# A graph layer and a mixture of experts on one core: row loads three blocks ahead, a bias add on VectorE, later router steps

## The chip, the cores and the metric

The kernel runs on one core of one Trainium2 chip. The metric is device time in microseconds (us) for one execution of the whole program; lower is better. Short names of engines, as the profile has them: PE is TensorE's matmul, PEld its weight load, DVE is VectorE, ACT is ScalarE, POOL is GpSimd, SP is SyncE (here it only issues DMAs and loads registers). L764 is line 764 of the kernel before.

## The reference

All data are float32. `x` has 6250 nodes of 256 features; 100000 edges with 96 features each are sorted by target node `dst`.

```python
# message passing and MLP, on h0 = layernorm(x)
out1 = segment_sum(edge_attr, dst, n)
out2 = where(cnt > 0, segment_max(edge_attr, dst, n), 0)
out3 = out1 / maximum(cnt, 1)
h = concatenate([h0, out1, out2, out3, u[0] for each node], axis=1)
h = relu(h @ W1 + b1) @ W2 + b2          # hidden size 1024, out 256
x = x + (h + h0)
# mixture of experts, on g = layernorm(x)
topk_vals, topk_idx = top_k(g @ gate_w + gate_b, 2)          # 16 experts
w = softmax(topk_vals)
moe = sum over the two chosen e of w_e * (relu(g @ w1[e] + eb1[e]) @ w2[e] + eb2[e])   # inner size 512
y = g + moe
x = x + layernorm(y) * gamma + beta
```

## The kernel before

**Groups and slots.** Nodes lie in 50 tiles of 125; four tiles make a group, 13 groups in all (group 0 has two tiles). A group is worked on in 12 slots. The order of all instructions is written by a planner: `at_slot(T, fn, ..., cost)` puts a step into slot T, the steps are then emitted in the order of their slots, and each engine works through its own queue in that order. In a slot PE has eight first-layer matmul parts (`hidden`, L764) or a second-layer output (`output`, L792). A slot of 4.6 us of VectorE time is filled up with pieces of the edge stream; the `cost` of a step is taken from what the stream may use. In the terms of the code, a step at `B + k` of group g lies in slot 12 g + k.

**Edge stream.** Chunks of edge columns are loaded by SP (`raw`, L176), VectorE runs a segmented sum and maximum over them (L316, L317, L319, L320, one 125x768 instruction each for a column), and SP stores the result (`rows_d`, L329). When a region of edges is done, `chain_runs` carries runs across rows and partitions: VectorE (L385 to L396), PE transposes (L404, L406), VectorE scans (L415 to L421), PE transposes (L430), VectorE (L436, L438), and a store of `carry_d` on GpSimd's queue (L440). A group's slot needs its region's edges first (`edges_until`).

**A group's way.** `take_x` loads its nodes, `stats_x`, `root_x`, `scale_x`, `norm_x` make the layer norm; `keep_x` scales `xt` on ScalarE (L714) and adds the second bias `b2b` on GpSimd (L716); `take_edges` and `take_carry` gather segment results with indirect DMAs of GpSimd (L722, L729); VectorE joins them (L735, L737), ScalarE masks them (L742); `turn` transposes on PE (L755). Then `hidden`, `output`, and `residual` on VectorE (L797). The router: `turn_b` (PE, L822), `logits` (PE, L830), `choose` (VectorE, L837 on), `rank` (VectorE, L851 to L858), `rank_2` (PE, L865 and L866), `place` (VectorE, L874 to L887) and `send`, eight indirect stores of GpSimd a group, which put each node's row into `xg_d` once for each of its two experts (L891). The PSUM pool `pG` that `logits`, `rank_2` and `bounds` use has one buffer.

**Bounds.** `bounds(b)` finds where each node's edges end: two VectorE instructions on sums that ScalarE made (L502), then two PE matmuls (L516, L517). It is called for parts of the nodes, before they are needed.

**Expert blocks.** 57 blocks of 256 rows are run one after the other; the first 14 belong to the most chosen expert and share one set of weights, the others have weights of their own (1026 KB each). `load_block(b)` has SP load two registers, the rows `xb` (L1028), and for most blocks the expert's second bias `eb` (L1033) and weights `wt` (L1035); buffers: seven for `xb`, three for weights. `run_block(b)` emits: `weigh` of block b-1 (VectorE L1077, ScalarE L1079, store of `y_d` on SP, L1081), `load_block(b+2)`, `finish` of an older block, four first-layer steps on PE (L1152) with relu on ScalarE (L1158), between them `turn_block(b+1)` (PE L1048), partners' rows gathered from `y_d` by GpSimd (L1090), statistics on VectorE, `norm_y`, and `norm_block(b+2)` on ScalarE, which is the first to read `xb` (L1041); last the second layer on PE (L1176). The last group's sends are emitted between the first blocks: two tiles' before block 5, two tiles' before block 6.

Of the kernel before, what the change touches and what calls it, by code (L numbers as in the profile page):

```python
# [14 lines left out]
OP = mybir.AluOpType  # L15
# [4 lines left out]
P = 125  # L20
PA = 80
RR = 8
GW = 2
# [14 lines left out]
SLOTS = 12  # L38
# [7 lines left out]
def kernel(  # L46
# [460 lines left out]
    def bounds(b):  # L507

        a, z = node_cols(b)
        n = z - a  # L510
        cols = slice(a, z)
        nc.vector.tensor_scalar(rp[:, cols], acc2[:, cols], float(KB), 0.5, op0=OP.add, op1=OP.mult)
        nc.vector.scalar_tensor_tensor(rp[:, cols], blk_f[:, cols], float(KB), rp[:, cols], op0=OP.mult, op1=OP.add)

        ends[b] = ps_e = pGp.tile([P, GS * NE], F32, name="pg")
        nc.tensor.matmul(ps_e[:, :n], sh, rp[:, cols], start=True, stop=False)  # L516
        nc.tensor.matmul(ps_e[:, :n], wrap, rp[:, a + 1:z + 1], start=False, stop=True)  # L517
# [191 lines left out]
    def keep_x(g):  # L709

        n = GRP[g][1] - GRP[g][0]
        xt = G[g]["xt"]
        for i in range(n):
            nc.scalar.activation(xt[:, i, 0:D], xt[:, i, 0:D], AF.Identity, scale=G[g]["rs1"][:, i:i + 1],  # L714
                                 bias=G[g]["nb"][:, i:i + 1])
        nc.gpsimd.tensor_tensor(xt[:, :n, 0:D], xt[:, :n, 0:D], b2b[:, None, :].to_broadcast([P, n, D]), op=OP.add)  # L716

# [202 lines left out]
    def open_experts():  # L920
# [3 lines left out]
        MB["pools"] = pools = ExitStack()  # L924
        for nm, bufs in (("tb", 1), ("wp", 3), ("xg", 7), ("bk", 3), ("yb", 4)):
            MB[nm] = pools.enter_context(tc.tile_pool(name=nm, bufs=bufs, side="right"))
# [91 lines left out]

    def load_block(b):
        if b < NA:  # L1020
            r = nc.sync.value_load(MB["tab_a"][0:1, b:b + 1], min_val=0, max_val=(NA - 1) * SB)
            e = nc.sync.value_load(star_i[0:1, 0:1], min_val=0, max_val=NE - 1) if b == 0 else None
        else:
            e = nc.sync.value_load(MB["tab"][0:1, 0, b - NA:b - NA + 1], min_val=0, max_val=NE - 1)
            r = nc.sync.value_load(MB["tab"][0:1, 1, b - NA:b - NA + 1], min_val=0, max_val=NE * N - SB)
        BL[b]["r"] = r
        BL[b]["xb"] = xb = MB["xg"].tile([128, 2, DR], F32, name="xb")
        nc.sync.dma_start(xb, xg_d[ds(r, SB), :].rearrange("(p h) d -> p h d", h=2))  # L1028
        if 0 < b < NA:
            BL[b]["wt"], BL[b]["eb"] = BL[0]["wt"], BL[0]["eb"]  # L1030
            return
        BL[b]["eb"] = eb = MB["wp"].tile([128, D], F32, name="eb")
        nc.sync.dma_start(eb, eb2[ds(e, 1), :].to_broadcast([128, D]))  # L1033
        BL[b]["wt"] = wt = MB["wp"].tile([128, WROW], F32, name="wt")
        nc.sync.dma_start(wt, wpack[ds(e * 128, 128), :])  # L1035
# [96 lines left out]
    def run_due(kind, fn, keep):  # L1132
        while len(due[kind]) > keep:
            fn(due[kind].pop(0))

    def run_block(b, end):
        xT, wt = BL[b]["xT"], BL[b]["wt"]
        run_due("weigh", weigh, 0)
        if b + 2 < end and "wt" not in BL[b + 2]:
            load_block(b + 2)  # L1140
        run_due("finish", finish, 0)
# [80 lines left out]
    for g, (a, z) in enumerate(GRP):  # L1222
        B, n = SLOTS * g, z - a
        if g:
# [9 lines left out]
            for i in range(n):  # L1234
# [4 lines left out]
                else:  # L1239
# [6 lines left out]
                    at_slot(min(2 * i + 5, SLOTS - 2), mean_window, g, i)  # L1246
            at_slot(B - (4 if g == GW else 7), keep_x, g)
            for k in range(DC):
                at_slot(B - (4 if g == GW else 6) + k, turn, g, k)
# [8 lines left out]
        at_slot(B + SLOTS + 1 - early, root_b, g)  # L1258
        at_slot(B + SLOTS + 2 - early, scale_b, g, cost=0.3)
        for k in range(DC):  # L1260
            at_slot(B + SLOTS + 1 + k, turn_b, g, k)
        at_slot(B + SLOTS + 3, logits, g)
        at_slot(B + SLOTS + 4, choose, g, cost=2.4)
        at_slot(B + SLOTS + 5, rank, g, cost=1.3)
        at_slot(B + SLOTS + 6, rank_2, g)
        at_slot(B + SLOTS + 7, place, g, cost=1.5)
        for i in range(n):
            at_slot(B + SLOTS + 8 + i // 2, send, g, i)
    T = SLOTS * (NG - 3) + 21
# [3 lines left out]
    for b in range(3):  # L1273
        at_slot(T + 4 + b, load_block, b)
    T = SLOTS * (NG - 1) + HC + GRP[-1][1] - GRP[-1][0]
# [11 lines left out]
    for b in range(GW, len(IB)):  # L1287
# [10 lines left out]
        T = max(0, SLOTS * sum(IB[:b]) - (9 if b == GW else 12))  # L1298
        at_slot(T, bounds, b, cost=0.4)
        at_slot(T + 1, index_nodes, b, cost=4.0)  # L1300
# [3 lines left out]
    def fill_rows():  # L1304

        nc.vector.memset(fill[:, D + 1:D + 5], 4.0 * NE * N)
        for h in range(SB // 128):
            nc.gpsimd.dma_start(xg_d.rearrange("(e n) d -> n e d", n=N)[h * 128:(h + 1) * 128],
                                fill[:, None, :].to_broadcast([128, NE, DR]))

    at_slot(4, fill_rows)
    at_slot(6, find_star)
# [107 lines left out]
    with tc.manual_schedule():  # L1420
        global_part()
        stats_x(0, 0)
        for t in reversed(range(a, z)):
            find_edge(t)
        bounds(0)
        index_windows(0)
        for i in range(z - a):
# [6 lines left out]
        norm_x(0)  # L1434
        bounds(1)
        index_windows(1)
        for h in range(2):
# [57 lines left out]
    with tc.If(nc.values_load(MB["more"][0:1, 0:1]) != 0):  # L1495
        with tc.manual_schedule():
            for b in range(NS, min(NB, NS + 3)):
                load_block(b)
            for b in range(NS, min(NB, NS + 2)):
# [44 lines left out]
```

## Time and profile before

| | |
|---|---|
| three runs | 1319.05, 1316.25, 1308.22 us; median 1316.25 |
| profiled execution | 1312.53 us; span 1310.6 us, mean granted PE clock 0.946 |
| busy share of the span | PE 86%, PEld 60%, DVE 74%, ACT 47%, POOL 46% |
| DMA | 261.25 MB, mean 199 GB/s |
| chain that ended last | PE 28%, DVE 25%, DMA 16%, issue 11%, ACT 6%, POOL 6%, SP 4% |
| largest waits | ACT L1041 for `xb`: 105.9 us; POOL L716 for ACT L714: 57.2 us |

A busy share is a mean over stages that have different limits, so the table says little about any one stage. A view by stretches of time tells which engine is full where. A line of groups or of the timeline has: start and length in us (timeline only), engine, source line, operation, tile written and tiles read, shape, count, and in square brackets the idle time of the engine just before, with what ended it. Matmul ends are modelled; starts are recorded.

### The profile page before, as it was taken

To read this page: it belongs to the slowest core of one execution; us is meant where nothing else is said; L and a number is where in the kernel's file an instruction comes from. 1 tells how busy PE (TensorE), PEld (TensorE's weight loads), DVE (VectorE), ACT (ScalarE), POOL (GpSimd) and SP (SyncE) were. 2 spreads that over 40 slices of the span, in tenths; PEclk is the share of its full clock that TensorE was granted. 3 is DMA by queue.
4 is the path that set the end of the run, shared out by engine and by line. 5 is a ranking of instruction groups with operands and counts; after the bars stand their busy time and mean duration, and the time that the engine had idled before them with its cause. 6 is when DMAs were issued, how large, how long until landed. Compare 5 with 4: busy or idle time off the path is not lost.

```text
span 1310.6 us, 16927 instructions
## 1 busy us (share of the span) xinstructions
PE 1125.1 (86%) x4637; PEld 788.1 (60%) x4637; DVE 970.5 (74%) x2741; ACT 617.8 (47%) x1449; POOL 602.0 (46%) x734
## 2 busy tenths in 40 slices
PE   2584696988989888999979999988999899999892
PEld 1353363646556454655636567866888777888771
DVE  4569787989989989999988522534468777888775
ACT  3474342643547442353333422422466666666662
POOL 4131152773578574637444513030045455564654
PEclk9897798998999888999998999998999999999996
DMA  5949775698699988899997221221577788888872
GB/s 162 216 110 229 216 220 156 182 299 230 176 236 274 251 251 217 223 264 236 267 268 195 67 82 33 65 82 49 181 214 227 231 255 257 263 243 259 259 254 73
DMA packets 179475, 261.25 MB, mean 199 GB/s; under 512 B 35915, under 2 KB 145963, under 8 KB 173729
## 3 DMA queue, kind: packets, MB, share of 16 engines
q1 hardware_dynamic: 140241, 202.23, 54.5%
q0 software_dynamic: 39008, 57.35, 15.8%
q8 instruction: 40, 0.66, 0.2%
q14 instruction: 74, 0.61, 0.1%
q10 hardware_dynamic: 112, 0.41, 0.1%
HBM read 146.70 MB, written 122.01 MB: 205 GB/s over the span
## 4 chain that ended last, share of the span: by engine, by line
PE 28%; DVE 25%; DMA 16%; issue 11%; ACT 6%; POOL 6%; SPq 4%; POOLq 0%; DVEq 0%; ACTq 0%
PE acc L1176 9%; PE acc L1152 8%; DMA rows_d<-rw 6%; PE acc L764 5%; DVE rw L317 3%; PE acc L792 3%; DMA xb<-xg_d 3%; DVE rw L320 3%; DMA xt<-in_x_dram 2%; DVE rw L319 2%; DVE rw L316 2%; ACT yb L1079 2%; POOL xg_d L891 2%; DVE yb L1077 2%; SPq L176 2%
## 5 line engine op out<-in xcount | busy, mean ns | idle before, releaser
L764 PE MATMUL acc<-inT,w1x 128*128 128x500 f32 (+1 forms) x832 | 375.2, 602 | 11.8 <-ACT hT L786 10.1
L764 PEld LDWEIGHTS acc<-inT,w1x 128*128 128x128 f32 x832 | 164.2, 205 | 175.2 <-issue 155.0
L1152 PE MATMUL acc<-xT,wt 128*128 128x256 f32 x912 | 224.3, 389 | 26.8 <-ACT hb L1158 22.2
L891 POOL DMA_INDIRECT xg_d<-xt,pos_i x100 | 156.7, 1567 | 160.5 <-DVE xt L887 87.7
L1176 PE MATMUL acc<-wt,hb 128*128 128x256 f32 x912 | 207.8, 381 | 0.0
L1152 PEld LDWEIGHTS acc<-xT,wt 128*128 128x128 f32 x912 | 169.8, 192 | 60.2 <-ACT hb L1158 35.7
L1176 PEld LDWEIGHTS acc<-wt,hb 128*128 128x128 f32 x912 | 174.7, 192 | 24.3
L792 PE MATMUL acc<-w2s,hT 128*125 128x256 f32 x800 | 180.8, 382 | 0.0
L792 PEld LDWEIGHTS acc<-w2s,hT 128*125 128x125 f32 x800 | 148.6, 189 | 23.0 <-issue 1.9
L1090 POOL DMA_INDIRECT g<-y_d,from_i x86 | 89.7, 1043 | 130.1 <-DMA y_d<-yb 94.0
L1123 POOL DMA_INDIRECT out_dram<-g,to_i x86 | 89.6, 1042 | 101.1 <-ACT hb L1158 77.2
L1041 ACT ACTIVATE xnb<-xb 128x256 f32<-128x256 f32 x114 | 62.1, 593 | 108.1 <-DMA xb<-xg_d 105.9
L495 POOL DMA_INDIRECT gb<-in_dst_dram,blk_i x50 | 72.8, 1456 | 85.8 <-DVE blk_i L492 44.4
L1158 ACT ACTIVATE hb<-acc,wt 128x256 f32<-128x256 f32 x200 | 87.8, 465 | 49.5 <-PE acc L1152 34.3
L786 ACT ACTIVATE hT<-acc,c 128x500 f32<-128x500 f32 (+1 forms) x104 | 60.3, 662 | 96.3 <-PE acc L781 96.3
L1077 DVE TENSOR_TENSOR yb<-acc,xe 128x512 f32<-128x512 f32 x57 | 39.4, 691 | 87.0 <-PE acc L1176 57.0
L756 ACT COPY inT<-pT 128x500 f32<-128x500 f32 (+1 forms) x65 | 36.4, 560 | 106.8 <-PE pT L755 91.1
L316 DVE TENSOR_TENSOR rw<-rw,keep 125x768 f32<-125x768 f32 x81 | 76.8, 949 | 12.3 <-DMA rows_d<-rw 9.5
L320 DVE TENSOR_TENSOR rw<-rw,raw 125x768 f32<-125x768 f32 x88 | 85.6, 972 | 0.0
L319 DVE TENSOR_TENSOR rw<-rw,raw 125x768 f32<-125x768 f32 x88 | 83.4, 948 | 0.0
L722 POOL DMA_INDIRECT at<-rows_d,first_i x44 | 60.9, 1385 | 46.8 <-issue 25.5
L317 DVE TENSOR_TENSOR rw<-rw,bar 125x768 f32<-125x768 f32 x81 | 81.3, 1004 | 0.0
(313 smaller groups left out, 1623.6 us busy)
## 6 DMA issues: line engine op xcount, KB each, us to landing
wt<-in_wpack_dram SPq DMA_DIRECT2D x44, 1026.0 KB
rows_d<-rw SPq DMA_DIRECT2D x46, 960.0 KB
rows_d<-rw SPq DMA_DIRECT2D x46, 540.0 KB
raw<-in_edge_dram SPq DMA_DIRECT2D x46, 480.0 KB
xb<-xg_d SPq DMA_DIRECT2D x57, 263.0 KB
y_d<-yb SPq DMA_DIRECT2D x57, 256.0 KB
raw<-in_edge_dram SPq DMA_DIRECT2D x46, 270.0 KB
xt<-in_x_dram SPq DMA_DIRECT2D x12, 500.0 KB
```

The source lines that it names most:

```text
L316: nc.vector.tensor_tensor(su, prev[0], keep[c][:, :, s + j, None].to_broadcast(bcast), op=OP.mult)
L317: nc.vector.tensor_tensor(mx, prev[1], bar[c][:, :, s + j, None].to_broadcast(bcast), op=OP.min)
L319: nc.vector.tensor_tensor(su, su, x_j, op=OP.add)
L320: nc.vector.tensor_tensor(mx, mx, x_j, op=OP.max)
L764: nc.tensor.matmul(G[g]["pH"][m % 4][:, :n * P], w1x[:, k, m * 128:(m + 1) * 128], inT[:, k, :n * P], start=(k == 0), stop=False)
L792: nc.tensor.matmul(pO, G[g]["hT"][m][:, i * P:(i + 1) * P], w2s[:, m, :], start=(m == 0), stop=(m == HC - 1))
L891: d = nc.gpsimd.indirect_dma_start(out=xg_d[:, :], out_offset=IndirectOffsetOnAxis(ap=G[g]["pos"][:, i, k:k + 1], axis=0), in_=G[g]["xt"][ ...
L1090: d = nc.gpsimd.indirect_dma_start(out=g[:, h, :].bitcast(I32), out_offset=None, in_=y_d[:, :], in_offset=IndirectOffsetOnAxis(ap=BL[b]["f ...
L1123: d = nc.gpsimd.indirect_dma_start(out=out[:, :], out_offset=IndirectOffsetOnAxis(ap=BL[b]["to"][:, h:h + 1], axis=0), in_=g[:, h, :], in_ ...
L1152: nc.tensor.matmul(pB[i][:, half, :], wt[:, k * FF + m * 128:k * FF + (m + 1) * 128], xT[:, k, :], start=(k == 0), stop=(k == DC - 1))
L1158: nc.scalar.activation(hb[:, m, :], pB[i][:, half, :], AF.Relu, bias=bias)
L1176: nc.tensor.matmul(pY[:, h, :], hb[:, m, h * 128:(h + 1) * 128], wt[:, W2O + m * D:W2O + (m + 1) * D], start=(m == order[0]), stop=(m == o ...
```

## The change

- `add_b2` is a step of its own on VectorE, two to three slots after `keep_x`, with a planned cost of 1.1 us; group 0's is in slot 2.
- `load_block` is split. `load_rows` (registers and `xb`) is called three blocks ahead, `load_weights` (`eb`, `wt`) two as before. The pool of `xb` and of small tiles has eight buffers instead of seven.
- For all groups but the last two, `logits`, `choose` and `rank` come one slot later, `rank_2`, `place` and `send` two.
- `bounds` is split: its two VectorE instructions come two slots earlier (for parts 3 to 5), its matmuls, now `bounds_2`, stay in their slot.

```diff
     def bounds(b):
...
         nc.vector.scalar_tensor_tensor(rp[:, cols], blk_f[:, cols], float(KB), rp[:, cols], op0=OP.mult, op1=OP.add)
 
+    def bounds_2(b):
+        a, z = node_cols(b)
+        n = z - a
+        cols = slice(a, z)
         ends[b] = ps_e = pGp.tile([P, GS * NE], F32, name="pg")
...
-        nc.gpsimd.tensor_tensor(xt[:, :n, 0:D], xt[:, :n, 0:D], b2b[:, None, :].to_broadcast([P, n, D]), op=OP.add)
+
+    def add_b2(g):
+        n = GRP[g][1] - GRP[g][0]
+        xt = G[g]["xt"]
+        nc.vector.tensor_tensor(xt[:, :n, 0:D], xt[:, :n, 0:D], b2b[:, None, :].to_broadcast([P, n, D]), op=OP.add)
...
-        for nm, bufs in (("tb", 1), ("wp", 3), ("xg", 7), ("bk", 3), ("yb", 4)):
+        for nm, bufs in (("tb", 1), ("wp", 3), ("xg", 8), ("bk", 3), ("yb", 4)):
...
-    def load_block(b):
+    def load_rows(b):
...
         nc.sync.dma_start(xb, xg_d[ds(r, SB), :].rearrange("(p h) d -> p h d", h=2))
+        BL[b]["e"] = e
+
+    def load_weights(b):
+        e = BL[b]["e"]
         if 0 < b < NA:
...
         run_due("weigh", weigh, 0)
+        if b + 3 < end and "xb" not in BL[b + 3]:
+            load_rows(b + 3)
         if b + 2 < end and "wt" not in BL[b + 2]:
-            load_block(b + 2)
+            load_weights(b + 2)
...
             at_slot(B - (4 if g == GW else 7), keep_x, g)
+            at_slot(B - (2 if g == GW else 4), add_b2, g, cost=1.1)
...
+        late = 0 if g >= NG - 2 else 1
         for k in range(DC):
             at_slot(B + SLOTS + 1 + k, turn_b, g, k)
-        at_slot(B + SLOTS + 3, logits, g)
-        at_slot(B + SLOTS + 4, choose, g, cost=2.4)
-        at_slot(B + SLOTS + 5, rank, g, cost=1.3)
-        at_slot(B + SLOTS + 6, rank_2, g)
-        at_slot(B + SLOTS + 7, place, g, cost=1.5)
+        at_slot(B + SLOTS + 3 + late, logits, g)
+        at_slot(B + SLOTS + 4 + late, choose, g, cost=2.4)
+        at_slot(B + SLOTS + 5 + late, rank, g, cost=1.3)
+        at_slot(B + SLOTS + 6 + 2 * late, rank_2, g)
+        at_slot(B + SLOTS + 7 + 2 * late, place, g, cost=1.5)
         for i in range(n):
-            at_slot(B + SLOTS + 8 + i // 2, send, g, i)
+            at_slot(B + SLOTS + 8 + 2 * late + i // 2, send, g, i)
...
-        at_slot(T + 4 + b, load_block, b)
+        at_slot(T + 4 + b, load_rows, b)
+        at_slot(T + 4 + b, load_weights, b)
...
-        at_slot(T, bounds, b, cost=0.4)
+        early = 0 if b == GW else 2
+        at_slot(T - early, bounds, b, cost=0.4)
+        at_slot(T, bounds_2, b)
...
+    at_slot(2, add_b2, 0)
```

More of the change, by code (lines that the diff above doesn't have):

```diff
@@ L1425 @@
         bounds(0)
+        bounds_2(0)
         index_windows(0)
@@ L1435 @@
         bounds(1)
+        bounds_2(1)
         index_windows(1)
@@ L1497 @@
             for b in range(NS, min(NB, NS + 3)):
-                load_block(b)
+                load_rows(b)
+                load_weights(b)
             for b in range(NS, min(NB, NS + 2)):
```

## The prediction

> **What bounds the kernel now.** I read the busy time by stretch first, because the shares of the page mix a message-passing stage (edges and MLP, to about 811 us) with an expert stage (57 blocks of rows after it). Columns: stretch, its length, busy time and count of PE, PEld, DVE, ACT, POOL, then granted clock, DMA share, GB/s.
>
> ```profile
> 100.00:690.00 590.00, 506.74 (x1887) 300.92 (x1885) 530.25 (x1370) 252.12 (x588) 314.72 (x272) 0.92 0.86 233
> 690.00:800.00 110.00, 110.00 (x432) 67.35 (x433) 52.19 (x182) 40.50 (x83) 43.05 (x53) 0.97 0.38 100
> 955.00:1310.60 355.60, 311.00 (x1463) 263.73 (x1461) 269.21 (x831) 218.13 (x494) 191.88 (x342) 0.97 0.74 231
> ```
>
> From 100 to 690 us DVE is busy 530 of 590 us and PE 507, at a clock of 0.92. As the waits of DVE in that stretch name PE for only some 4 us, while PE's name DVE again and again, DVE leads there and PE follows. From 690 to 800 PE is busy without a gap. After 955 PE is busy most of the time again, and DVE and ACT are not full.
>
> Next, the order of time around one GpSimd add (L716, the second bias), and PE's last long wait before it runs free:
>
> ```profile
> 628.70 2.17 POOL L716 TENSOR_TENSOR xt<-xt,b2b 125x1024 f32<-125x1024 f32 x1 [8.92 <-ACT xt L714]
> 628.84 2.68 DVE L858 TENSOR_TENSOR M<-M,mm 125x16 f32<-125x16 f32 x4
> 631.44 0.95 DVE L319 TENSOR_TENSOR rw<-rw,raw 125x768 f32<-125x768 f32 x1
> ...
> 689.94 0.65 PE L865 MATMUL pg<-mm,before 125*125 125x64 f32 x2 [8.03 <-DVE mm L856]
> 690.48 0.68 PE L866 MATMUL pg<-M,ones 125*125 125x64 f32 x2
> 690.95 1.04 PE L755 MATMUL pT<-ident,xn 125*128 125x125 f32 x4
> 691.79 5.59 PE L764 MATMUL acc<-inT,w1x 128*128 128x500 f32 x8
> 697.31 1.12 PE L781 MATMUL acc<-inT,w1r 32*128 32x500 f32 x8
> 698.36 0.65 PE L755 MATMUL pT<-ident,xn 125*128 125x125 f32 x4
> 698.85 7.07 PE L792 MATMUL acc<-w2s,hT 128*125 128x256 f32 x32
> ```
>
> The four L858 adds on 125x16 take 2.68 us, elsewhere about 0.8: the first alone takes 2.05 us and ends with the GpSimd add. And eight L764 matmuls behind PE's 8 us wait take 5.6 us; in other places the same eight take 3.5.
>
> Last, two expert blocks on PE (a block is L1152 x8, L1048 x4, L1152 x8, L1176 x16):
>
> ```profile
> 1204.76 1.99 PE L1152 MATMUL acc<-xT,wt 128*128 128x256 f32 x8
> 1206.59 3.62 PE L1176 MATMUL acc<-wt,hb 128*128 128x256 f32 x16
> 1210.05 1.89 PE L1152 MATMUL acc<-xT,wt 128*128 128x256 f32 x8
> 1212.30 0.33 PE L1048 MATMUL pT<-ident,xnb 128*128 128x128 f32 x1 [0.37 <-ACT xnb L1041]
> 1212.80 0.55 PE L1048 MATMUL pT<-ident,xnb 128*128 128x128 f32 x3 [0.17 <-ACT xnb L1041]
> 1214.14 1.99 PE L1152 MATMUL acc<-xT,wt 128*128 128x256 f32 x8 [0.79 <-ACT hb L1158]
> 1215.97 3.62 PE L1176 MATMUL acc<-wt,hb 128*128 128x256 f32 x16
> ```
>
> This block takes 9.38 us from L1176 to L1176; an unbroken one takes 7.72. ACT had waited 3.40 us for xb, and what stands behind that on ACT (weigh, relu) came late for PE.
>
> **The second bias.** Removed from GpSimd: 13 adds of 1.2 to 2.8 us. Laying them over DVE's instructions, 11 of the 13 have one DVE instruction that ends with the add instead of after its usual time (L858 2.05 us for 0.17, L317 3.32 for 0.95, L735 2.63 for 0.31). The ten of groups 2 to 11, at 183 to 686 us, take 19.4 us from DVE in this way. Added to DVE: 768 elements take 0.95 us and 512 take 0.69 (L1120), so 1.01 ns an element; 1024 take 1.21 us, and ten of them 12.1. Net on DVE: 7.3 us less. The add of group 0 (0.69) and group 1 (1.21) fall before 105 us, where DVE waits for ACT (8.5, 6.0 and 3.5 us at L602): nothing, 1.9 if that cover is gone. Group 12's lies at about 745 us, where PE is the bound and DVE half idle: nothing.
>
> The Trainium skill ("SBUF — State Buffer", section "Who interferes with whom") says that VectorE with two SBUF inputs and a GpSimd instruction that reads SBUF exclude one another for the whole instruction, whoever comes first; the trace agrees, with 19.4 us over ten adds. Against the change, "Perfetto Trace Analysis" ("Optimizing Scalar/DVE Operations") holds that work may be taken off a saturated VectorE, even to GpSimd, though the shared port can spoil it; by its first half alone DVE would lose 12.1 us here instead of winning 7.3.
>
> The add waits for ACT's L714, with all of DVE's queue behind it (edges, then the matmuls that need residuals). Group 10's L714 ends at 628.6, and DVE's joins of its slot pass at 641.9: 13 us of margin. Only group 2 has none (both at 182.5): at most 1 to 2 us once. GpSimd's own wait for L714 (57.2 us in all) goes; behind it stood gathers with 15 to 20 us of slack (issued by 672, joined at 692), so it's worth nothing.
>
> **TensorE's router parts later.** For all but the last two groups logits, choose and rank move one slot (4.6 us by the plan), rank_2, place and the eight sends two. On PE the L865 pair moves past L755, L764 x8, L781, L755 and sixteen of L792, some 9 us of full-speed work, while DVE's rank moves about one slot: some 4.5 us of slack. The sends move two slots back in GpSimd's queue, ahead of the gathers still: of the 20 us of slack some 11 are left; if it were used up, joins would wait as one did at 470 us (4.1). The bounds are split: DVE's two instructions go two slots (9 us) ahead of PE's; the ACT sums that they read end at 302.3 and 479.5 for use at 319.7 and 497.3, so this is covered. PE's waits there (3.5 and 7.8 us, and 9.5 at 156.8 where logits held the bank) I cost at nothing, since PE still meets DVE later: at 661 us its transposes wait 0.51 us for DVE's residual. With DVE no longer leading they would be worth up to 20.8 us.
>
> What counts is PE's time at 690 us. DVE is earlier there by nine hits (17.4 us) less nine adds (10.9): 6.5 us, and has the 4.5 us of slack on top, so the 8.0 us wait and the slow matmuls after it (2 us) go, unless DMA holds DVE. Going the other way, the built order has the last edge chunk's three PE steps (L404, L406, L430) one right behind the other, where before 7.9 us lay between the first and the last; DVE's scans between them took 1.6 us (720.4 to 722.0): a new wait of 2 us on PE's unbroken run. Bounds: 14 us gained (all of PE's side) to 5 lost (no gain, the new wait, a half-clock 3 us). I take 9 less 2: **7 us**. PE's clock in the records is 0.5 for 3.4 to 13.7 us at each longer wait, here 685.7 to 695.9; "TensorE: Matmul & The Clock Gate" of the Trainium skill (section "What's actually happening") describes such halving after an idle window of about 3.4 us.
>
> **Rows three ahead.** Each block issues the same row load and, from block 14 on, the same two register loads on SP, in the same place of SP's queue (behind the y_d store, ahead of the weights), but for a block one later; the bytes are the same. With eight buffers the load reuses that of block b-5, finished in block b-2: no new wait. So xb, which now lands 2.5 to 5 us after its issue and some 1 to 3 us after ACT wants it (105.9 us of ACT waits in 52 blocks), has one block, 7.7 us, more.
>
> - Blocks 0 to 13: two loads stand behind the last group's sends (ACT waits 8.66 and 9.46 us); PE stands still 3.2 and 2.3 us in these blocks, and runs at half clock for 3.4 us (866.6): 1.7 more. With a block more xb lands (863.5 and 875.6) about when ACT wants it: **7 us**. If the sends came 8 us later, nothing.
> - Blocks 14 to 56: blocks with an xb wait of 1.9 us or more run 1.42, 0.29, 0.24, 0.41, 0.23, 1.66, 1.32, 1.06, 1.22 and 0.91 us over 7.72, together 8.8. Nine others (22 to 26, 28, 29, 33, 34) run 0.84 over it for another reason: DVE's L1077 starts 4.50 us after the first L1176 instead of 3.65, with xb no later than in clean blocks. One in four of the recovered blocks may fall into that: **6 us**. Below: if all blocks fell into it, 32 x 0.84 = 27 us lost; above, 16 won.
>
> **The sum.** 7 + 7 + 6 = 20 us off the profiled execution (1312.5 us, span 1310.6): 1292.5. That execution lies 3.7 us under the median of the three runs (1316.25; they go from 1308 to 1319), so the median becomes 1296.
>
> **Rivals.**
> - DMA takes over before 690 us. For it: DMA share 0.98 at 385 to 440 and 660 to 692 us, rows_d stores 13 us in the chain. Against: DVE waits for them only 9.5 us in all. Then only the expert parts count: 13 us, 1303.
> - The add costs DVE its full 12.1 us and the relief does not come, because other GpSimd instructions catch DVE. For it: one DVE instruction beside a descriptor instruction of GpSimd took 1004 ns for 950. Against: that is 0.05 us, not 2. Then 12 lost, 13 won: 1315. The first half of the rule on trace analysis above would give this.
> - Slower: the late start of L1077 spreads, as ACT's xnb now runs a microsecond earlier in each block. For it: it is unexplained, and comes in rows. Against: block 17, with no xb wait, was clean. It decides from 24 blocks more (20/0.84); in all 32 it costs 27 us against 20: 1323, and with less won before it, over 1329.
> - The change does not do what it says: rows still late, as SP itself is late. For it: xb is issued 2 us behind the y_d store. Against: that is far under a block. Then 14 us less is won: 1310.
>
> **How the numbers follow.** Forecast 0.55 (its own range 1283 to 1308), DMA 0.17, full price 0.10, late start 0.12, rows still late 0.06. Runs of this kernel differ by some 0.4% either way, so about 1% is what can be told from no change. Under 1303: 0.53 of the forecast and 0.07 of DMA, 0.60. Over 1329: 0.03 of full price and 0.09 of late start, 0.12. The range 1282 to 1322 leaves out the worst of the late start and a greater gain.
>
> **What would show it.** Right: no L716 on POOL, twelve adds of 1.2 us and one of 0.7 on DVE; no L858 or L735 of 2 us; PE's wait for rank before its free run under 4 us, and the waits for bounds nearly gone; a new wait of about 2 us at L430; ACT's waits for xb under 40 us; blocks 5, 6 and 47 to 54 at 7.5 to 7.8 us. Wrong: DVE's waits for rows_d stores grown by as much as the adds gave; expert blocks of 8.5 us in more than half of the rows; or the last L792, now at 809.6 us, not earlier than 806.

## The result, and the profile after

| | before | after |
|---|---|---|
| median of four runs beside each other | 1315.99 us | 1298.58 us (1289.16 to 1302.38) |
| ratio, with its 95% interval | | 0.9863 (0.9821 to 0.9906) |
| profiled execution, span | 1312.53, 1310.6 us | 1299.43, 1297.6 us |
| second layer of block 0 starts (MLP stage over) | 815.6 us | 809.0 us |
| from there to block 14 | 126.4 us | 118.8 us |
| from block 14 to block 56 | 340.2 us | 341.1 us |

The changed kernel is 1.4% faster. The last three rows are read from starts in the trace: the MLP stage ends 6.5 us earlier, blocks 0 to 13 give 7.6 us, and blocks 14 to 56, where the prediction expected 6 us, lose 0.9. Line numbers after the change are 8 higher in the MLP part (L764 became L772, L792 L800, L865 L873) and 12 to 14 higher in the expert blocks (L1077 became L1089, L1152 L1166, L1176 L1190).

The busy time by stretch, with the same columns as for the kernel before:

```profile
100.00:690.00 590.00, 509.79 (x1911) 302.78 (x1910) 525.66 (x1388) 252.63 (x590) 280.77 (x262) 0.93 0.85 233
690.00:800.00 110.00, 107.36 (x434) 67.92 (x433) 51.66 (x181) 38.02 (x79) 41.73 (x59) 1.00 0.40 109
955.00:1310.60 355.60, 297.07 (x1404) 253.12 (x1402) 260.19 (x799) 205.16 (x474) 188.52 (x333) 0.97 0.70 221
```

DVE (third busy figure) does 18 instructions more in the first stretch and is busy 4.6 us less, and PE gets 24 matmuls further. GpSimd (fifth) is busy 34 us less. Over the whole span DVE fell from 970.5 to 963.4 us, although it now has the thirteen adds. The last stretch is no longer full of blocks, since the kernel ends in it.

Around one add, and around the place of PE's 8 us wait:

```profile
638.57 0.95 DVE L317 TENSOR_TENSOR rw<-rw,bar 125x768 f32<-125x768 f32 x1
639.44 1.22 DVE L724 TENSOR_TENSOR xt<-xt,b2b 125x1024 f32<-125x1024 f32 x1
640.58 0.95 DVE L319 TENSOR_TENSOR rw<-rw,raw 125x768 f32<-125x768 f32 x1
...
688.29 0.65 PE L763 MATMUL pT<-ident,xn 125*128 125x125 f32 x4 [1.54 <-ACT inT L764]
688.78 3.62 PE L800 MATMUL acc<-w2s,hT 128*125 128x256 f32 x16
692.23 0.33 PE L873 MATMUL pg<-mm,before 125*125 125x64 f32 x2
...
718.59 0.43 PE L430 MATMUL ps<-ident,st 96*125 96x96 f32 x2 [1.73 <-DVE st L421]
```

The add takes 1.22 us between two edge instructions at their usual length. L873, the old L865, has no bracket: the wait for rank is gone. The new wait at L430 is 1.73 us.

The waits of the whole execution: engine and line, what it waited for, us in total, times, longest:

```profile
ACT dv L853 <- DVE dv L852: 79.3, 11, 16.2
DVE at L743 <- DMA cg<-carry_d,next_i: 30.6, 18, 5.4
PE pT L763 <- ACT inT L764: 30.2, 12, 7.7
PE pg L520 <- DVE rp L513: 21.9, 5, 8.7
ACT xnb L1053 <- DMA xb<-xg_d: 6.7, 2, 5.7
```

Before, the same waits read (the bounds' have two rows there):

```profile
ACT dv L845 <- DVE dv L844: 38.0, 10, 8.2
DVE at L735 <- DMA cg<-carry_d,next_i: 10.9, 5, 4.6
PE pT L755 <- ACT inT L756: 9.5, 6, 6.5
PE pg L516 <- DVE rp L513: 22.9, 4, 8.9
PE pg L516 <- DVE lg L837: 9.5, 1, 9.5
ACT xnb L1041 <- DMA xb<-xg_d: 105.9, 52, 9.5
```

The waits for rows are nearly gone. The waits for the bounds are halved where the change moves them: 9.48, 3.50 and 7.81 us became 4.83, 2.56 and 3.21; the rest of those rows, 11.6 and 11.3 us, falls before 100 us, where nothing was moved. Three others have grown: ScalarE's router exponent waits for DVE, ScalarE's copies of transposed inputs stand behind it, and PE waits for those copies; and DVE waits longer for the gathers (L743).

Last, one expert block of this execution, and below it one of a second execution of the same kernel (told of further down):

```profile
1075.20 3.62 PE L1190 MATMUL acc<-wt,hb 128*128 128x256 f32 x16
1078.66 1.89 PE L1166 MATMUL acc<-xT,wt 128*128 128x256 f32 x8
1079.75 0.69 DVE L1089 TENSOR_TENSOR yb<-acc,xe 128x512 f32<-128x512 f32 x1 [1.54 <-PE acc L1166]
1080.48 0.91 ACT L1091 ACTIVATE yb<-yb,w_b 128x256 f32<-128x256 f32 x2 [2.64 <-DVE yb L1089]
1081.48 0.81 ACT L1172 ACTIVATE hb<-acc,wt 128x256 f32<-128x256 f32 x2
1081.98 1.99 PE L1166 MATMUL acc<-xT,wt 128*128 128x256 f32 x8 [1.00 <-ACT hb L1172]
1083.81 0.59 PE L1190 MATMUL acc<-wt,hb 128*128 128x256 f32 x2
```

```profile
1063.56 3.62 PE L1190 MATMUL acc<-wt,hb 128*128 128x256 f32 x16
1067.01 1.89 PE L1166 MATMUL acc<-xT,wt 128*128 128x256 f32 x8
1067.21 0.69 DVE L1089 TENSOR_TENSOR yb<-acc,xe 128x512 f32<-128x512 f32 x1 [0.92 <-PE acc L1190]
1067.94 0.91 ACT L1091 ACTIVATE yb<-yb,w_b 128x256 f32<-128x256 f32 x2 [1.74 <-DVE yb L1089]
1068.94 0.81 ACT L1172 ACTIVATE hb<-acc,wt 128x256 f32<-128x256 f32 x2
1069.44 2.00 PE L1166 MATMUL acc<-xT,wt 128*128 128x256 f32 x8
1071.28 3.62 PE L1190 MATMUL acc<-wt,hb 128*128 128x256 f32 x16
```

In both, PE runs L1190 without a gap and goes on with L1166 3.45 us after its start. In the second block DVE reads the result 3.65 us after that start; in the first (block 32) only after 4.55. The bracket of the first names L1166, not L1190, because the semaphore by which PE releases DVE moves there at 4.52 us and again, for L1166, 0.06 us later; in a clean block of the same execution (35) it moves at 3.63 us. The two scalings (L1091) wait for DVE, the relus (L1172) stand behind the scalings on ScalarE, and PE's second half of L1166 waits 1.00 us for the relus. So the block lasts 8.61 instead of 7.72 us. I call this a late start. Nineteen of blocks 14 to 55 have it here (22 to 26, 28 to 34, 37 to 43); in the execution before there were nine up to block 34.

### The profile page after: what moved, and what is told of

Same layout as the page of the kernel before. It is cut to its first block, busy times and chain, and to the rows that moved or that the text cites. A ratio compares the mean times of both kernels' runs of the same rounds, so it can differ in the third digit from the quotient of the medians.

```text
span 1297.6 us, 16883 instructions
## 1 busy us (share of the span) xinstructions
PE 1113.4 (86%) x4637; PEld 783.4 (60%) x4637; DVE 963.4 (74%) x2754; ACT 612.6 (47%) x1449; POOL 558.8 (43%) x721
## 3 DMA queue, kind: packets, MB, share of 16 engines
q0 software_dynamic: 39008, 57.35, 16.1%
## 4 chain that ended last, share of the span: by engine, by line
PE 35%; DVE 13%; ACT 3%; DMA 3%; issue 3%; POOL 1%; POOLq 0%; SPq 0%; ACTq 0%; DVEq 0%
PE acc L1190 14%; PE acc L1166 11%; PE acc L772 5%; PE acc L800 3%; DVE yb L1089 2%; ACT yb L1091 2%; DVE rw L320 1%; DVE rw L317 1%; DVE rw L319 1%; DVE rw L316 1%; DMA xt<-in_x_dram 1%; ACT hb L1172 1%; DMA cg<-carry_d,next_i 1%; DMA xg_d<-xt,pos_i 1%; POOL xg_d L899 1%
## 5 line engine op out<-in xcount | busy, mean ns | idle before, releaser
L772 PE MATMUL acc<-inT,w1x 128*128 128x500 f32 (+1 forms) x832 | 369.0, 592 | 8.9 <-DVE xt L805 8.9
L772 PEld LDWEIGHTS acc<-inT,w1x 128*128 128x128 f32 x832 | 159.0, 199 | 169.7 <-issue 151.9
L1166 PE MATMUL acc<-xT,wt 128*128 128x256 f32 x912 | 223.2, 388 | 29.3 <-ACT hb L1172 25.7
L899 POOL DMA_INDIRECT xg_d<-xt,pos_i x100 | 134.4, 1344 | 250.2 <-DVE xt L895 119.8
L1190 PE MATMUL acc<-wt,hb 128*128 128x256 f32 x912 | 207.1, 380 | 0.0
L1166 PEld LDWEIGHTS acc<-xT,wt 128*128 128x128 f32 x912 | 169.2, 191 | 62.3 <-ACT hb L1172 38.1
L1190 PEld LDWEIGHTS acc<-wt,hb 128*128 128x128 f32 x912 | 174.1, 191 | 23.9
L800 PE MATMUL acc<-w2s,hT 128*125 128x256 f32 x800 | 186.5, 388 | 0.0
L800 PEld LDWEIGHTS acc<-w2s,hT 128*125 128x125 f32 x800 | 150.5, 193 | 23.7 <-issue 1.9
L1091 ACT ACTIVATE yb<-yb,w_b 128x256 f32<-128x256 f32 x114 | 51.7, 501 | 154.0 <-DVE yb L1089 147.8
L495 POOL DMA_INDIRECT gb<-in_dst_dram,blk_i x50 | 74.1, 1483 | 114.2 <-issue 59.4
L1172 ACT ACTIVATE hb<-acc,wt 128x256 f32<-128x256 f32 x200 | 87.7, 464 | 49.5 <-PE acc L1166 41.0
L1089 DVE TENSOR_TENSOR yb<-acc,xe 128x512 f32<-128x512 f32 x57 | 39.4, 691 | 88.3 <-PE acc L1190 57.4
L317 DVE TENSOR_TENSOR rw<-rw,bar 125x768 f32<-125x768 f32 x81 | 77.0, 950 | 0.0
L730 POOL DMA_INDIRECT at<-rows_d,first_i x44 | 61.6, 1399 | 34.2 <-issue 21.5
L737 POOL DMA_INDIRECT cg<-carry_d,next_i x44 | 63.2, 1437 | 25.7 <-issue 11.3
```

Of the source, the lines that this page charges most:

```text
L317: nc.vector.tensor_tensor(mx, prev[1], bar[c][:, :, s + j, None].to_broadcast(bcast), op=OP.min)
L772: nc.tensor.matmul(G[g]["pH"][m % 4][:, :n * P], w1x[:, k, m * 128:(m + 1) * 128], inT[:, k, :n * P], start=(k == 0), stop=False)
L800: nc.tensor.matmul(pO, G[g]["hT"][m][:, i * P:(i + 1) * P], w2s[:, m, :], start=(m == 0), stop=(m == HC - 1))
L899: d = nc.gpsimd.indirect_dma_start(out=xg_d[:, :], out_offset=IndirectOffsetOnAxis(ap=G[g]["pos"][:, i, k:k + 1], axis=0), in_=G[g]["xt"][ ...
L1166: nc.tensor.matmul(pB[i][:, half, :], wt[:, k * FF + m * 128:k * FF + (m + 1) * 128], xT[:, k, :], start=(k == 0), stop=(k == DC - 1))
L1172: nc.scalar.activation(hb[:, m, :], pB[i][:, half, :], AF.Relu, bias=bias)
```

## Experiments

The table holds all kernels that ran. "Late" counts the blocks of 14 to 55 whose L1089 starts 4.3 us or more after the first second-layer matmul. Columns three to six are from one profiled execution each. "Rows", "add" and "slots" are the change's parts: rows three ahead, second bias on VectorE, and later router steps with split bounds. "Relus first" is an edit of mine, in the first experiment. A few blocks are counted as late only because PE itself paused in them (29 of "before again", 49 of "rows", 41 of "after + relus first").

Each ratio is to runs of the kernel before made beside it; it is not the quotient of the two medians (for rows, 1296.56 over 1318.52 us would be 0.983). Rows, add, slots and "after + relus first" ran on one chip (number 5 of the record), the other experiments on another (14); for the first profiles of before and after the chip is not on record.

| kernel | ratio to before (95%) | block 0 at | 0 to 14 | 14 to 56 | late |
|---|---|---|---|---|---|
| before, first profile | | 815.6 | 126.4 | 340.2 | 10 |
| before again | 0.9991 (0.9968 to 1.0013) | 816.7 | 127.8 | 343.2 | 1 |
| after, first profile | 0.9863 (0.9821 to 0.9906) | 809.0 | 118.8 | 341.1 | 19 |
| after again | 0.9772 (0.973 to 0.9814) | 812.3 | 119.0 | 325.2 | 0 |
| rows | 0.9873 (0.9814 to 0.9932) | 814.3 | 118.9 | 330.1 | 3 |
| add | 1.0044 (1.0003 to 1.0086) | 819.6 | 128.2 | 343.4 | 7 |
| slots | 1.0075 (1.0046 to 1.0103) | 824.9 | 128.7 | 347.3 | 12 |
| before, loads ahead of store | 0.9905 (0.9876 to 0.9935) | 818.4 | 128.6 | 325.2 | 0 |
| after + relus first | 0.9654 (0.9605 to 0.9702) | 815.0 | 114.2 | 316.5 | 4 |
| the same once more | 0.9644 (0.9594 to 0.9693) | 809.6 | 113.8 | 308.1 | 0 |
| rows + relus first | 0.9649 (0.9618 to 0.968) | 819.5 | 112.0 | 308.6 | 1 |
| rows + add + relus first | 0.9714 (0.9686 to 0.9743) | 823.3 | 115.4 | 308.1 | 1 |
| rows + slots + relus first | 0.9739 (0.971 to 0.9769) | 832.1 | 115.1 | 308.1 | 1 |
| after + relus first + exponent later | 0.9645 (0.9611 to 0.9679) | 813.0 | 113.9 | 308.1 | 0 |

### Relus ahead of the scalings

```diff
 def weigh(b):
...
     nc.vector.tensor_tensor(yb, BL[b]["pY"], xe, op=OP.add)
+
+def scale_y(b):
+    yb = BL[b]["yb"]
     for h in range(2):
         nc.scalar.activation(yb[:, h, :], yb[:, h, :], AF.Copy, scale=BL[b]["w"][:, h:h + 1])
...
             else:
                 nc.scalar.activation(hb[:, m, :], pB[i][:, half, :], AF.Relu, bias=bias)
+        if half == 0:
+            run_due("scale", scale_y, 0)
         if half == 0 and b + 1 < end:
             turn_block(b + 1)
```

> The changed kernel with one thing more: in an expert block ScalarE's two scalings of the block before (and the store of its rows) are issued behind the four relus of the first half and no longer ahead of them; VectorE's add of the second layer's result stays where it is. Theory: a late-start block costs 0.84 us because the scalings, which wait for that late add, stand ahead of the relus that TensorE's second half waits for; with the relus first the 19 blocks of 8.55 us become blocks of 7.7: about 16 us faster than the changed kernel, some 1283 us. Rival: the late release of the second layer's result itself holds TensorE (through the accumulator that it must give back), so the blocks stay at 8.55 and the time within 3 us of the changed kernel. Rival: the store comes too late for the gathers of partner rows, which then hold stats and finish: blocks longer, slower by over 5 us.

Measured: median 1273.91 us, 0.9654 of before, against 0.9863 for the changed kernel: 2.1% less, more than the 16 us expected. Against the second set of runs of the changed kernel (0.9772, below) it is 1.2%. One block of the profile, at 7.35 us:

```profile
1092.75 3.62 PE L1196 MATMUL acc<-wt,hb 128*128 128x256 f32 x16
1094.61 0.07 SPq L1036 DMA_DIRECT2D xb<-xg_d  x1
1096.21 1.89 PE L1170 MATMUL acc<-xT,wt 128*128 128x256 f32 x8
1096.41 0.69 DVE L1089 TENSOR_TENSOR yb<-acc,xe 128x512 f32<-128x512 f32 x1 [0.54 <-PE acc L1196]
1097.27 0.47 ACT L1176 ACTIVATE hb<-acc,wt 128x256 f32<-128x256 f32 x1 [1.08 <-PE acc L1170]
1098.37 1.89 PE L1170 MATMUL acc<-xT,wt 128*128 128x256 f32 x8
1098.51 0.90 ACT L1094 ACTIVATE yb<-yb,w_b 128x256 f32<-128x256 f32 x2
1099.43 0.36 SPq L1096 DMA_DIRECT2D y_d<-yb  x1
1100.10 1.24 PE L1196 MATMUL acc<-wt,hb 128*128 128x256 f32 x5
```

The first relu (L1176) starts 4.52 us into the block instead of 5.38, as soon as PE has given it its operands, and PE no longer pauses. So even the clean block of 7.72 us had held 0.37 us of this wait; 42 blocks of 0.37 are 15.5 us beside the 16 of the late starts. Two executions without late starts show this part alone: 325.2 us from block 14 to 56 without the edit, 308.1 with it. For the late starts themselves the evidence is thin, as this profile has few: blocks 38 and 49, whose L1089 starts 4.41 and 4.32 us in, take 7.51 and 7.35 us, as the theory has it, but block 33, at 5.50, takes 9.16. So the theory holds as far as it was tested, and its price left out the clean blocks. Block 41 takes 13.61 us: ScalarE's relus there wait 3.01 us for a release, and PE stands 3.22 us for them.

### The changed kernel again, and before again

> The changed kernel once more, nothing edited: how much of what its one profile showed is the program and how much that execution. Theory (late starts belong to the program): again about 19 late blocks, the same ones (22 to 26, 28 to 34, 37 to 43), first second-layer matmul of block 0 within 2 us of 809, time 1294 to 1302. Rival (they belong to the execution): another set of late blocks, anything from 2 to 25 of them, and the time moves with their number by 0.84 us each.

> The kernel before once more, unchanged, for a second profile of it. Theory: late starts differ from execution to execution (the changed kernel showed 19 in one, none in another), so here another set than 22 to 26, 28, 29, 33, 34; block 0 at 816 within 4; blocks 5 and 6 at 11 to 12 us and the waits for rows of 38 to 55 again, since these belong to the program. Rival: the same late blocks.

The late starts are not the program's alone: the changed kernel has 19 in one profile and none in the other, and the kernel before has ten (nine up to block 34, and 48) and one (29). Between the two profiles of the changed kernel the stretch from block 14 to 56 differs by 15.9 us, and 19 times 0.84 is 16.0. The two ratios, 0.9863 and 0.9772, have intervals that do not meet, which suggests that runs that lie together are alike in this.

Whether it is the execution or the chip was not tried. The eight profiles from chip 14 have at most one late block each, the four from chip 5 have 3, 7, 12 and 4, and no kernel was profiled twice on one chip that the record names. That late starts come and go between executions on one chip is therefore not shown. What makes PE's release late was not found.

Blocks 5 and 6 (12.87 and 10.73 us long) and the waits for rows in blocks 38 to 54 came back in the second profile of before, so they are the program's. With one late block only, the rows' waits were larger, 123.4 us for 105.9, and stretched blocks from 22 on (22, 28 and 42 to 9.25, 10.79 and 9.16 us).

### The three parts alone

> Of the change only the expert part: rows three blocks ahead, weights two, xg eight deep; the second bias stays on GpSimd, the router and bounds stay where they were. Theory: the expert part owes nothing to the rest, so this kernel gains what the changed kernel gained between the first second-layer matmul and the end: 7.6 us in blocks 0 to 13, nothing to -1 in blocks 14 to 56, together 6 to 7 us faster than before, with blocks 5 and 6 at 7.5 us and again about 19 blocks of 8.55 us (late start) behind block 14. Rival A: the late start depends on how the MLP part ended; with 9 such blocks as before the gain is 14 to 15 us. Rival B: rows loaded earlier cost the loads of weights their turn in the queue; then blocks 14 to 56 lose more than 5 us and the whole is no faster than before.

> Of the change only the second bias: added on VectorE in the slots of the changed kernel, router, bounds and expert loads as before. Theory (locked-out VectorE): the ten adds between 100 and 690 us cost VectorE 12 us and free it of the 19.4 us in which GpSimd's add held one of its instructions; the first second-layer matmul of block 0 comes 5 to 8 us earlier than before, and the expert part stays as it was: 5 to 8 us faster. Rival (full price): the held instructions were covered by other waits, and VectorE's 12 us come on top: 5 to 12 us slower. Rival (nothing moves): the MLP part is led by TensorE and loads, and the add is within 2 us either way, so the 6.5 us that the changed kernel gained before block 0 come from the router's slots.

> Of the change only the slots: logits, choose, rank, rank_2, place and send one or two slots later, bounds split in two; second bias on GpSimd, expert loads as before. Theory: the wait of 8 us at 690 us becomes 2 us, but the later sends push the gathers (VectorE waited 30.6 us for them in the changed kernel, 10.9 before) and the later exponent holds ScalarE's copies (TensorE waited 30.2 us for them, 2.0 before), so that nothing is left: first second-layer matmul of block 0 from 2 us earlier to 5 us later, whole kernel -2 to +5 us. Rival: the slots carry the gain of the MLP part: 5 to 8 us faster. If this kernel and the one with only the add both stay within 2 us of before, the 6.5 us need both.

Rows alone are as fast as the whole change in its first runs (0.9873; 1296.56 us), though not as in its second (0.9772). Their profile has the 7.6 us of blocks 0 to 13, and 10.2 us more behind block 14 with three late blocks: more gain and fewer late blocks than even rival A had (14 to 15 us, nine). The change's own first profile had lost that to its late starts.

By the ratios add alone and slots alone are slower than before, by 5.8 and 9.9 us of the median of before in those runs (1318.52); the interval of the add alone, 1.0003 to 1.0086, is only just clear of no change. Both theories of mine were wrong on these: the add by itself follows the "full price" rival in its time, though not in its ground, since VectorE's busy time fell by 7.4 us; and the slots cost more than foreseen. The waits that the theory of the slots named hardly came. For the gathers DVE waited, with the add alone and with the slots alone:

```profile
DVE at L739 <- DMA cg<-carry_d,next_i: 23.4, 15, 4.6
DVE at L739 <- DMA cg<-carry_d,next_i: 13.9, 9, 4.4
```

The kernels with neither have 10.9 to 18.6 us there, so what raised this wait in the changed kernel came with the add and not with the later sends. PE's waits for the copies are 13.5 us with the slots alone, 9.5 with neither or with the add, and 30.2 only with both.

To be rid of the late starts the two were tried again on top of rows and relus first:

> Only rows three ahead, and the scalings behind the relus, on the kernel before: second bias on GpSimd, router and bounds as before. Beside the changed kernel with the scalings moved (0.965 of before) it prices the two MLP edits together, without late starts. Theory (the MLP edits are worth the 6.5 us by which block 0 came earlier in the profiles): 5 to 8 us slower than that kernel, 0.970. Rival (their worth is within what executions differ, since the scalings' kernel has the same MLP part and started block 0 at 815.0): within 3 us of it, 0.963 to 0.968. Rival (add and slots cost what they did alone, 5.8 and 9.9 us): 10 us or more faster, below 0.958.

> The kernel with rows three ahead and the scalings moved (0.965 of before, block 0 at 819.5), and of the MLP edits only the second bias on VectorE. Theory (VectorE is freed of more than the adds cost): block 0 at 811 to 815, the whole 3 to 8 us faster, 0.959 to 0.963. Rival (full price): block 0 at 823 or later, 4 us or more slower, 0.968 and up. Rival (adds and lock cancel, as the mean of the profiles cannot exclude): within 2 us.

> The same kernel, and of the MLP edits only the later router slots and the split bounds. Theory (alone the slots hold up gathers and copies while VectorE still carries the lock): block 0 at 821 to 826, 2 to 9 us slower, 0.967 to 0.972. Rival (the slots carry the MLP part's gain): block 0 at 813 or earlier, 5 us faster, 0.961.

There the base is 0.9649, the add makes it 0.9714, the slots 0.9739, both together 0.9654 and 0.9644. So of the pair the rival "within 3 us" came true, of the add alone the full price (block 0 at 823.3), and the slots alone are slower than their theory (832.1). Alone each costs (0.65 and 0.90% of 1316 us: 8.6 and 11.8 us); together they cost, and bring, nothing that the whole times can tell. In the profiles block 0 starts at a mean of 816.9 us in five profiles with neither (814.3 to 819.5), at 811.5 in four with both (809.0 to 815.0), at 821.4 in two with the add, at 828.5 in two with the slots. So in the MLP stage the pair is worth some 5.4 us, and the sum of the parts, 4.5 and 11.6 lost, is wrong by 21.5. Why these 5.4 us are not in the whole times is open; blocks 0 to 13 took 2 us less without the pair (112.0, against 114.2 and 113.8).

The trace shows one thing in which the pair and each part alone differ. From the kernel with rows, the add and relus first, in SP's queue and then on DVE and PE (L516 is the first matmul of the bounds, L686 the first read of a group's nodes):

```profile
484.04 1.55 SPq L176 DMA_DIRECT2D raw<-in_edge_dram  x2
485.64 1.60 SPq L329 DMA_DIRECT2D rows_d<-rw  x2
487.60 1.26 SPq L676 DMA_DIRECT2D xt<-in_x_dram  x1
...
505.68 0.43 DVE L686 BATCH_NORM_STATS2 bsa<-xt 125x6 f32<-125x256 f32 x1 [9.05 <-DMA xt<-in_x_dram]
...
515.20 0.18 DVE L513 SCALAR_TENSOR_TENSOR rp<-blk_f,rp 125x20 f32<-125x20 f32 x1
515.43 0.61 PE L516 MATMUL pg<-rp,sh 125*125 125x20 f32 x2 [16.33 <-DVE rp L513]
```

The same load in the kernel before:

```profile
466.15 1.00 SPq L676 DMA_DIRECT2D xt<-in_x_dram  x1
```

There 62 edge loads (L176) stood ahead of it on SP; here 64 do, which wait for DVE to give back their buffers, and it goes out 21 us later (16 us later than with rows and relus first alone, 471.8 us with 62 ahead). DVE then stands still 9.05 us for it, with residuals and bounds queued behind, and PE stands 16.33 us, where it stood 7.8 before. With the add alone on before it is the same (484.8 us, 64 ahead, 8.8 and 16.1 us). With the slots alone 64, 74, 82 and 92 edge loads stand ahead of four such loads that had 62, 72, 80 and 90 before, and DVE waits 6.0 and 7.0 us for the second. With both the counts are 62, 72, 80 and 90 again; only one load, at 360 us, has 44 for 42, and DVE waits 5.0 us for it. So the planned costs and slots move pieces of the edge stream across the loads of nodes in SP's queue. That the counts are back is seen; that they are the cause was not tried, since no kernel moves the loads of nodes alone.

### The order of loads and store

```diff
-        run_due("weigh", weigh, 0)
         if b + 2 < end and "wt" not in BL[b + 2]:
             load_block(b + 2)
+        run_due("weigh", weigh, 0)
```

> The kernel before with two calls of run_block in the other order: the loads of the block two ahead are issued ahead of the store of the last block's rows, which waits for ScalarE's scalings, and no longer behind it; nothing three ahead. Theory (rows came late because their load stood on SP's queue behind the store, issued at 6.3 to 9.5 us of a block; ahead of it at 1.2 to 2.3, as in the kernels with the scalings moved): blocks 5 and 6 and 38 to 55 lose their waits for rows, ScalarE's waits for rows fall from 105.9 to under 25 us, 10 to 18 us faster than before, as rows three ahead alone. Rival (a third block ahead is needed, the scalings' kernel hid the waits by other slack): waits for rows stay over 60 us and the time within 5 us of before.

Measured: 1301.08 us, 0.9905 of before. ScalarE's waits for rows, of this kernel and of before in the second profile:

```profile
ACT xnb L1041 <- DMA xb<-xg_d: 18.6, 2, 10.1
```

```profile
ACT xnb L1041 <- DMA xb<-xg_d: 123.4, 51, 9.8
```

All the waits behind block 14 are gone, with no buffer and no third block ahead: that stretch takes 325.2 us, the same as the changed kernel again. The load of block b+2's rows no longer stands behind the store that waits for ScalarE's scalings of block b-1: it is issued between 1.7 us before and 0.7 us after the start of that block's second layer, where it came 7.1 to 9.1 us after it, so some 8 us earlier. Of the expectation the two blocks 5 and 6 were wrong: they still take 12.6 and 12.4 us. The rows that ScalarE reads in them are those of blocks 7 and 8. These loads are issued 4.1 and 16.6 us after the second layer of block 5 began, when the last group's sends (the last of each four starts at 0.3 and 12.3 us) have landed. With rows three ahead, block 7's rows are loaded ahead of the sends, 8.9 us before that point, and block 8's 4.4 us after it, behind the first four sends but a block before they are read; only block 9's load still stands behind the last sends, and blocks 5 and 6 take 7.53 us.

### The exponent later

```diff
 def choose(g):
...
-    nc.scalar.activation(dv[:, :n], dv[:, :n], AF.Exp)
...
 def rank_2(g):
+    nc.scalar.activation(dv[:, :n], dv[:, :n], AF.Exp)
```

> The changed kernel with the scalings behind the relus, and the router's exponent issued one step later on ScalarE, ahead of rank_2's matmuls and no longer in choose. Theory: ScalarE's wait for the exponent's input (79 us in the changed kernel, 16 the longest) is what holds the copies of the transposed inputs, for which TensorE waited 30 us there and 2 us before; with it gone TensorE's waits at that line fall below 10 us and block 0 starts 5 to 15 us earlier than in the kernel with the scalings alone (1274): 1260 to 1270. Rival: TensorE would have waited for something else of the same slots (VectorE's additions, the gathers), and the time stays within 3 us.

Measured: 1269.77 us, 0.9645, no faster than the two runs of the same kernel without this edit (0.9654 and 0.9644). The waits changed places:

```profile
PE pT L763 <- ACT at L750: 13.6, 13, 2.7
PE pT L763 <- ACT inT L764: 12.3, 10, 6.5
PE pg L873 <- DVE mm L863: 4.5, 2, 3.6
```

PE's waits for the copies fell from 30.2 us in the changed kernel (33.9 and 34.1 in the two profiles of this kernel without the edit) to 12.3, as the theory had it in kind, and the longest, 7.7 us at 351 us, became 3.6 us of waiting for rank (L873) in the same place. Block 0 at 813.0 lies among the others, 809.6 and 815.0. The rival is right about the time. That DVE leads there, so that PE meets it at the next line, is my reading of the wait that moved.

### Rows under the relus-first order

> The changed kernel without its part on rows (rows and weights both two ahead, xg seven deep), with the scalings behind the relus: prices the rows without late starts. Theory: the waits for rows come back, in blocks 0 to 13 some 7 us (blocks 5 and 6 at 11 to 12 us) and 8 to 12 us in blocks 38 to 55: 15 to 19 us slower than the same kernel with rows three ahead, 1289 to 1293. Rival: a shorter block (7.35 us instead of 7.72) needs rows sooner, so that the waits grow: 25 us or more slower. Rival: the space that the moved scalings give covers the waits: under 8 us slower.

The edit did not reach this kernel: what ran has rows three ahead and is the relus-first kernel once more. It gives that kernel a second time, 1266.33 us, and nothing on rows: what they are worth under the new order was not tried.

### The fastest

The kernel with all of the change and relus first is the fastest run, level with the one that has only rows and relus first: 0.9654 and 0.9644 against 0.9649. Both beat the kernel before by 3.5%, and the changed one (0.9863 and 0.9772) by 1.2 to 2.2%.

## Why the prediction was right, and where it was wrong

**The sum** of 7 + 7 + 6 made 1296 us; 1298.6 came, and 1287.4 in the second set of runs. In the profiled executions the gain was 13.1 us for 20, and all that lacks is in the third term; the first two were sound in size, the first of them partly by luck, as told below.

**The second bias.** VectorE's net of 7.3 us less: its busy time fell by 7.1 us with the whole change and by 7.4 with the add alone (963.1). Each add took 1.22 us for the 1.21 foreseen. So on VectorE's busy time the row weighs more than the rule of "Perfetto Trace Analysis" ("Optimizing Scalar/DVE Operations") in the Trainium skill, by whose first half VectorE would have lost 12.1 us. The step that failed is from busy time to time: with the add alone block 0 comes 4.5 us later, between the means. The edit moves edge loads ahead of a load of nodes in SP's queue, for which DVE then waits 9 us; the part on the add named VectorE's and GpSimd's queues but not SP's. That this wait is the whole of the loss was not tried.

**Router later.** The wait at 690 us went, and 2 us of new wait at L430 were 1.73. DVE's waits for the gathers rose from 10.9 to 30.6 us, but not by the later sends, whose slack of "some 11" us held: with the slots alone they are 13.9 us, with the add alone 23.4. The add's account had the gathers at "nothing"; why it brings these waits was not tried. That the waits for the bounds would be nearly gone was half right: 20.8 us at the three moved parts became 10.6. They had been costed at nothing, and no run here says otherwise. ScalarE's queue was left out: the later exponent waited 79.3 us for DVE, and the copies behind it made PE wait. With the exponent later still, those waits fell by some 22 us and the time did not, so they cost nothing that the times can tell. The term of 7 us (6.5 in the profile, 5.4 between the means, none in the whole times) has the size of the pair in the MLP stage, but the two halves were taken as two gains, and alone each is a loss. So the account of the 7 us, two gains that add up, was wrong, and that the size came out is partly luck.

**Blocks 0 to 13.** 7 us predicted, 7.6 measured, 7.6 again with rows alone. Blocks 5 and 6 took 7.53 us, and the waits for rows fell to 6.7 us where under 40 was asked.

**Blocks 14 to 56.** This is the term that failed: 6 us predicted, 0.9 lost. Of the 8.8 us called recoverable some 7.4 were recovered (340.2, less nine late starts of 0.84, less the 325.2 of the stretch with neither wait), but ten more blocks started late, 8.4 us. The step "One in four of the recovered blocks may fall into that" made the late start a price of the recovery, and it is none: the second execution of the same program, with its rows as early, had no such block. Without late starts, in two profiles from one chip, the rows are worth twice what was read, 343.2 to 325.2 us, 18; that the nine late starts in the profile that was read had given the rows time is the likely reason, not a tested one. The rival of the late start had the place and the price of a block right; its ground, that ScalarE's xnb runs earlier, fell with the second execution, with rows alone (three late) and with the loads ahead of the store (none). What does bring late starts stays open, the chip included.

**The other rivals.** DMA did not take over: DVE's waits for the rows_d stores fell from 9.5 to 4.9 us. Rows did not stay late. GpSimd's other instructions did not take the relief back, which was the ground of the full price: VectorE's busy time fell by 7 us.

## What to carry to other kernels

A step that is cheap by busy time can be dear by queue order: count, for each load in a shared queue, how many instructions stand ahead of it before and after, and try the parts of a change alone, since two losses may cancel. Where one engine's queue puts work that waits for a late result ahead of work that another engine needs now, exchange the two; here that was worth about as much as the whole change. And a price read from one profile holds for that execution: take a second profile, and one from another chip, before a repeated wait is called the program's.

## What was not expected of the hardware

The release of PE's last second-layer matmul reached VectorE either 3.65 us or about 4.5 us after the layer began, in the same program, for runs of blocks, and with PE's own matmuls equally dense; in one execution 19 of 42 blocks had it and in another none. In all 19, PE's semaphore moved for that layer at 4.42 to 4.52 us, and 0.05 to 0.08 us later for the first matmuls of the next, which in a clean block release at 4.49: the late release came only when the next was due. Runs of five late blocks or more are in the first profiles of before and after and in two of the four from chip 5; the eight from chip 14 have none. Once, with relus first, ScalarE was released more than 3 us after PE's matmuls had ended, by their modelled ends. No experiment here says why.
